# A four-layer graph network on one core: exps turned in 32x32 blocks by VectorE and brought to their keys' partitions by transfers

## The chip, the core and the metric

One core of a Trainium2 chip runs the whole program in a single launch. The metric is the device time of one execution in microseconds (us), as the median of several runs. The engines are TensorE (PE; its weight loads are listed as PEld), VectorE (DVE), ScalarE (ACT), GpSimd (POOL) and SyncE (SP), which here only issues transfers.

## The reference

x is (32, 512, 256) in fp32 and adj (32, 512, 512) in int32, the same adjacency for all four layers. Every layer adds to x a function of `h = max(layernorm(x), 0)`:

```python
# layer 0: 8 heads of 32
normed = layer_norm(h, gamma1, beta1)                       # q = k = v = normed, per head
attn = softmax(where(adj > 0, q @ k.T / sqrt(32), -inf))
h = h + attn @ v
out = h + gelu(layer_norm(h, gamma2, beta2) @ W1 + b1) @ W2 + b2
# layers 1 and 2: 4 heads of 64 (graph attention)
logits = leaky_relu(src_i + dst_j)                          # src, dst: one number per token and head
out = softmax(where(adj > 0, logits, very small)) @ (h @ W)
# layer 3: 4 heads of 64
q, k, v = h @ Wq + bq, h @ Wk + bk, h @ Wv + bv
out = relu(softmax(where(adj | eye, q @ k.T / 8, min)) @ v @ Wo + bo)
```

The 32 batches are independent of each other.

## The kernel before

**Work of a batch.** A batch holds its 512 tokens as four chunks of 128 partitions (token `c * 128 + q` in chunk c, partition q). Layers 0 and 3 share the helpers `attend` and `unit`. `attend` loops over two halves of the queries and over groups of heads (G = 4 heads in layer 0, G = 2 in layer 3, so that a group fills 128 partitions of q and k). For each chunk of 128 queries it issues the score products `dots` (L1078) into PSUM tiles pss, two heads in each, and then one `unit` per head:

- `masked` (L1125, VectorE): adds the mask to the 128x512 scores, negates, writes them to an SBUF tile e and keeps the row minimum in low;
- `exps` (L1137, ScalarE): the exp in place, with its row sum;
- `turn` (L1143, TensorE): four 128x128 transpositions of e into a PSUM tile pst, so that keys come to the partitions;
- `evacuate` (L963, VectorE or ScalarE): copies pst into eT.

When both query chunks of a half are there, `product` (L1099, TensorE) multiplies eT with the values into pso, and the `finish` of the layer divides by the row sums. A batch has 32 units in layer 0 and 16 in layer 3, 1536 in the whole run.

Layers 1 and 2 (`gat_layer`, `gat_attend`, `head_pair`, `gat_exps`) work with keys on partitions from the start; they need the mask transposed once per batch (maskT: `turn` in `batch`, L1747, four bf16 transpositions per chunk into psmT, copied out by VectorE at L1757). Their row maxima (junk, L1260) are VectorE's, their leaky exps (psu, e: L1446, L1467) ScalarE's, their sums over keys (esum, L1371) GpSimd's. Layer 0 ends with an MLP (psf L1528, psg L1549).

**Loads.** SP issues one transfer per 128 rows of adj (L1715, into one of two adj buffers), one for x (L1733) and one for the result (L1777). GpSimd turns each adj tile into a bf16 mask (L1720); this is done once for layers 0 to 2 and once more for layer 3.

**What sets the order.** All pieces of work are `Op`s of a `Plan`. Each has an engine (or a choice of two), a cost in the code, the buffers it needs and its predecessors. `Plan.schedule` places them one at a time: always the piece that can start first, and among those that can start at the same time the one with the smallest key. Up to four batches are in flight (FLIGHT). The finished list fixes each engine's instruction order; on the chip the engines only wait for each other by semaphores. The key is

```python
o.key = o.b * PACE + min(o.b, CHAINS - 1) * RAMP - o.cp - URGENCY.get(o.kind, 0.0)
fine = FINE.get(o.kind, ())
o.key -= fine[o.nth] if o.nth < len(fine) else 0
```

where cp is the longest path to the end and URGENCY and FINE are tables of numbers per kind of piece and per piece of a kind.

**Buffers.** PSUM: four tiles of one bank (tag one, for pst, pso and nearly all else) and two tiles of two banks (tag two: pss and psu). SBUF: six E tiles of 8 KB a partition (eT, the exps of layers 1 and 2, the MLP's hidden values), eight e tiles of 2 KB.

Of the kernel before, what the change touches and what calls it, by code (L numbers as in the profile page):

```python
# [9 lines left out]
F32 = mybir.dt.float32  # L10
# [6 lines left out]
P = 128  # L17
# [10 lines left out]
PACE = 24.3  # L28

RAMP = 466.5  # L30

LATENCY = {"PE": 0.25, "DVE": 0.18, "ACT": 0.26, "POOL": 0.15, "SP": 3.5}
TABLE_LOAD = 1.3

SWITCH = 150.8

SKEW = {"DVE": 0.07, "ACT": 0.0}
E_UNITS = 8

URGENCY = {  # L40
    "0:attend.dots:pss": 462.9,
    "0:attend.product:pso": -175.4,
    "0:batch:x": 178.5,
    "0:divide.scale:od": 938.2,
    "0:divide.turn:psd": 415.4,
    "0:divide:rc": 799.1,
    "0:evacuate:eT": 821.7,
    "0:evacuate:oT": -725.9,
    "0:finish.residual:h": -329.4,
    "0:layer0.down:psg": 1019.5,  # L50
    "0:layer0.rest:h": -1654.6,
    "0:layer0.up:psf": 35.3,
    "0:layer0:gT": 744.2,
    "0:layer0:h": -787.8,
    "0:layer0:x": 858.2,
    "0:mask_rows:adj": -575.2,
    "0:mask_rows:mask": -375.4,
    "0:moments.combine:mv": 317.1,
    "0:moments:st": 585.1,
    "0:norm:n": -2315.9,  # L60
    "0:norm:y": 27.1,
    "0:norm_relu:h": 451.8,
    "0:transposed.affine:qT": -614.7,
    "0:transposed.affine:yT": 1599.0,
    "0:transposed.turn:ps": 842.1,
    "0:unit.exps:e": -287.5,
    "0:unit.masked:e": 695.6,
    "0:unit.turn:pst": 906.7,
    "1:batch.turn:psmT": -364.5,
    "1:batch:maskT": -56.9,  # L70
    "1:divide.scale:od": 656.7,
    "1:divide.turn:psd": 1795.9,
    "1:divide:rc": -399.6,
    "1:evacuate:esum": -106.0,
    "1:evacuate:hT": 267.4,
    "1:evacuate:oT": -390.5,
    "1:gat_attend.key_terms:terms": 120.6,
    "1:gat_attend.maximum:grt": -949.2,
    "1:gat_attend:psd": 493.9,
    "1:gat_exps.leaky:psu": 254.7,  # L80
    "1:gat_exps.less:psu": 1557.1,
    "1:gat_exps.logits:psu": 232.7,
    "1:gat_exps:e": 1404.4,
    "1:gat_layer.project:psv": 1864.8,
    "1:head_pair.add:esum": 1941.4,
    "1:head_pair.product:pso": -781.0,
    "1:head_pair.sums:psz": 1214.9,
    "1:head_pair.turn:pst": -702.1,
    "1:head_pair:x": -1263.8,
    "1:largest.leaky:glz": 257.7,  # L90
    "1:largest:head": 34.7,
    "1:largest:most": 515.6,
    "1:largest:psm": 616.6,
    "1:largest:psn": 719.1,
    "1:moments.combine:mv": 1347.0,
    "1:moments:st": -193.6,
    "1:norm_relu:h": 564.8,
    "1:query_terms.terms:psw": 625.5,
    "1:rows_of.turn:psr": 520.6,
    "1:rows_of:rows": 297.3,  # L100
    "1:transposed.turn:ps": -474.0,
    "2:batch:mask": 20.7,
    "2:divide.scale:od": 1020.3,
    "2:divide.turn:psd": -785.5,
    "2:divide:rc": 718.1,
    "2:evacuate:esum": 268.7,
    "2:evacuate:hT": 67.8,
    "2:evacuate:oT": 2309.3,
    "2:gat_attend.key_terms:terms": 203.2,
    "2:gat_attend.maximum:grt": -1980.4,  # L110
    "2:gat_attend:psd": -581.1,
    "2:gat_exps.leaky:psu": -55.6,
    "2:gat_exps.less:psu": 277.3,
    "2:gat_exps.logits:psu": -221.2,
    "2:gat_exps:e": -803.2,
    "2:gat_layer.project:psv": -61.6,
    "2:head_pair.add:esum": 1765.9,
    "2:head_pair.product:pso": 275.0,
    "2:head_pair.sums:psz": -327.3,
    "2:head_pair.turn:pst": 571.6,  # L120
    "2:head_pair:x": 797.9,
    "2:mask_rows:adj": -580.1,
    "2:mask_rows:mask": -1055.3,
    "2:moments.combine:mv": 1499.2,
    "2:moments:st": 649.2,
    "2:norm_relu:h": -939.1,
    "2:query_terms.terms:psw": 256.8,
    "2:rows_of.turn:psr": 587.2,
    "2:rows_of:rows": -334.9,
    "2:transposed.turn:ps": 157.5,  # L130
    "3:attend.dots:pss": -1153.0,
    "3:attend.product:pso": -176.0,
    "3:batch:": -158.3,
    "3:evacuate:eT": -518.7,
    "3:evacuate:hT": -758.1,
    "3:evacuate:oT": 1394.4,
    "3:finish.spread:od": -316.9,
    "3:finish.turn:psr": 9.0,
    "3:finish:qT": -219.8,
    "3:finish:rc": -224.7,  # L140
    "3:layer3.biased:kT": 1662.2,
    "3:layer3.biased:qT": -462.4,
    "3:layer3.project:psk": -1285.4,
    "3:layer3.project:psq": 440.8,
    "3:layer3.project_v:psv": -300.3,
    "3:moments.combine:mv": 105.4,
    "3:moments:st": 752.7,
    "3:norm_relu:h": -4275.8,
    "3:project_out.add:x": 1996.5,
    "3:project_out.project:psw": -1291.9,  # L150
    "3:transposed.turn:ps": 397.0,
    "3:unit.exps:e": -287.1,
    "3:unit.masked:e": 592.5,
    "3:unit.turn:pst": -698.3,
}

FINE = {
    "0:attend.dots:pss": (
        26, 2, -1, -1, -1, -1, -36, -36,
    ),  # L160
    "0:attend.product:pso": (
        -123, -169, 83, -178,
    ),
    "0:batch:x": (
        30,
    ),
    "0:divide.scale:od": (
        5, -254, -116, 388,
    ),
    "0:divide.turn:psd": (  # L170
        -194, 3, -165, -57,
    ),
    "0:divide:rc": (
        -124, 16, -118, 9,
    ),
    "0:evacuate:eT": (
        0, -217, 4801, -188, 371, 176, 143, -381, 37, 119, 230, 185, 57, -46, -86, 139, -81, -15,
        223, -45, 59, -43, 177, 455, 45, -17, -12, 2, 25, -194, 118, -6,
    ),
    "0:evacuate:oT": (  # L180
        6, 84, -133, -26,
    ),
    "0:finish.residual:h": (
        -12, -60, -96, -130,
    ),
    "0:layer0.down:psg": (
        -80, -151, -109, 6,
    ),
    "0:layer0.rest:h": (
        -34, 51, -126, 13,  # L190
    ),
    "0:layer0.up:psf": (
        124, -172, -156, 145, -173, 64, -297, -184,
    ),
    "0:layer0:gT": (
        -105, -49, 42, -9, 115, -86, -50, 7,
    ),
    "0:layer0:h": (
        110, -95, -64, 31,
    ),  # L200
    "0:layer0:x": (
        13, 9, 37, 114,
    ),
    "0:mask_rows:adj": (
        -4, -1, 12, -36,
    ),
    "0:mask_rows:mask": (
        70, -58, -121, 69,
    ),
    "0:moments.combine:mv": (  # L210
        -12, 20,
    ),
    "0:moments:st": (
        -19, -48, 23, -89, -154, -179, -239, -171, -32, -164, -105, -82,
    ),
    "0:norm:n": (
        -4532, -4538, -4519, -4571,
    ),
    "0:norm:y": (
        -117, -26, -164, -223,  # L220
    ),
    "0:norm_relu:h": (
        -168, -276, -195, -261,
    ),
    "0:transposed.affine:qT": (
        -815, -106,
    ),
    "0:transposed.affine:yT": (
        361, 38,
    ),  # L230
    "0:transposed.turn:ps": (
        -593, -649, -208, -165,
    ),
    "0:unit.exps:e": (
        494, -41, 21, -71, -27, 264, 218, 1016, 80, -106, -66, -162, 18, -91, -63, -176, -53, 134,
        -47, -92, -85, -50, 167, 121, -99, -45, -70, -121, 50, 34, 55, -28,
    ),
    "0:unit.masked:e": (
        -10, -64, -87, -127, -385, -377, -391, -364, -60, -51, -7, -38, -165, -9, -142, 70, -29,
        -58, -31, -2, -78, -76, -40, -75, -4, 22, 20, 24, -118, -106, -28, -24,  # L240
    ),
    "0:unit.turn:pst": (
        -297, -422, -738, -401, -276, -253, -299, 296, 57, -188, 1, 62, -272, -298, 2, -35, -239,
        18, -238, -77, -117, -76, -36, -95, -133, -226, -214, -405, 89, -29, -208, -143,
    ),
    "1:batch.turn:psmT": (
        -17, 24, -128, -32,
    ),
    "1:batch:maskT": (
        2, -7, -50, 19,  # L250
    ),
    "1:divide.scale:od": (
        66, 88,
    ),
    "1:divide.turn:psd": (
        -665, -335,
    ),
    "1:divide:rc": (
        77, -7,
    ),  # L260
    "1:evacuate:esum": (
        -42, -22,
    ),
    "1:evacuate:hT": (
        19, 208, 73, -51, 41, 40,
    ),
    "1:evacuate:oT": (
        -81, -866,
    ),
    "1:gat_attend.key_terms:terms": (  # L270
        366,
    ),
    "1:gat_attend.maximum:grt": (
        19, 112, 80, 37, 18, -14, -6, 45, 61, -61, -21, 15, 7, 119, 26, 192,
    ),
    "1:gat_attend:psd": (
        -20, -173, -151, -188,
    ),
    "1:gat_exps.leaky:psu": (
        13, 172, -144, 229, 52, -342, -1019, -556,  # L280
    ),
    "1:gat_exps.less:psu": (
        -174, -58, -153, -180, -381, -613, 79, 311,
    ),
# [1532 lines left out]
```

## Time and profile before

| | |
|---|---|
| median of 3 runs | 5228.39 us (5225.8 to 5230.76) |
| the profiled execution | 5227.27 us, its span 5225.5 us, granted TensorE clock 0.991 |
| PEld busy | 2810.8 us |
| POOL busy | 2709.7 us (52%) |
| exps, L1137 on ACT | 1536, 1102.5 us busy, mean 724 ns |
| esum, L1371 on POOL | 384, of which 256 take 602.2 us, mean 2359 ns |
| mask from adj, L1720 on POOL | 256, 494.2 us busy, mean 1931 ns |
| mask turned, L1747 on PE | 512, 44.5 us busy |
| issues of x, adj and out on SP | 32, 256 and 32 |

Busy times are those of one profiled execution. The span runs from the first to the last instruction of the core; the execution's own time lies 1.77 us above it. Matmuls are pipelined, so their durations overlap: the busy time of a group is the union, its mean duration is that of a single one, and neither alone is what an instruction costs in a dense stream. A line number can be that of a helper: all copies out of PSUM made by `evacuate` have L963.

### The profile page before, as it was taken

Reading aid. Unit: us, or ns where it says so; the run is one execution under the profiler, and the core shown is the slowest. Engines: PE = TensorE matmul, PEld = TensorE weight load, DVE = VectorE, ACT = ScalarE, POOL = GpSimd, SP = SyncE. Lnnn points to the kernel's source line nnn. Section 1 sums busy time; section 2 is a strip of 40 time slices with the busy share of each in tenths; the row PEclk is TensorE's granted clock in tenths of the full one; section 3 lists DMA queues with packets and bytes.
Section 4 is the critical chain, followed back from the end, with each engine's and each line's share of the span. In section 5 each row is a group of like instructions: output and inputs, shape, how many; then the busy total and the mean of one; then the engine's idle time right before and its main releaser. Section 6 shows DMA issues by size and latency. Waiting matters only on the chain.

```text
span 5225.5 us, 86599 instructions
## 1 busy us (share of the span) xinstructions
PE 5085.6 (97%) x30972; PEld 2810.8 (54%) x30972; DVE 3163.1 (61%) x9219; ACT 3668.6 (70%) x7053; POOL 2709.7 (52%) x3988
## 2 busy tenths in 40 slices
PE   6989999999999999999999999999999999999998
PEld 4544555555555555555555555555555555555554
DVE  5545666666565666565666666665656665666653
ACT  6747777777677777677776667776777766677755
POOL 6445544565544655445655445654446554456442
PEclk9989999999999999999999999999999999999999
DMA  2000000000000000000000000000000000000000
GB/s 84 1 9 25 20 10 21 25 25 25 17 11 23 25 25 25 11 15 25 25 25 19 11 21 25 25 25 15 13 23 25 25 25 15 11 25 25 13 13 13
DMA packets 78692, 110.31 MB, mean 21 GB/s; under 512 B 9523, under 2 KB 45238, under 8 KB 78262
## 3 DMA queue, kind: packets, MB, share of 16 engines
q1 hardware_dynamic: 70656, 100.68, 6.4%
q8 instruction: 246, 4.03, 0.3%
q10 hardware_dynamic: 7606, 4.08, 0.3%
q14 instruction: 184, 1.51, 0.1%
HBM read 87.97 MB, written 16.78 MB: 20 GB/s over the span
## 4 chain that ended last, share of the span: by engine, by line
PE 76%; POOL 13%; DVE 5%; ACT 3%; issue 2%; DMA 0%; ACTq 0%; POOLq 0%; SPq 0%; DVEq 0%
PE pst L1143 12%; PE pss L1078 9%; PE psg L1549 8%; PE psf L1528 8%; PE pso L1099 8%; POOL esum L1371 6%; PE psv L1574 4%; PE pso L1385 4%; PE psu L1441 3%; POOL mask L1720 2%; PE psk L1597 2%; PE psv L1625 2%; DVE junk L1260 2%; PE psq L1597 2%; PE psu L1433 2%
## 5 line engine op out<-in xcount | busy, mean ns | idle before, releaser
L1137 ACT ACTIVATE e<-e,low 128x512 f32<-128x512 f32 x1536 | 1102.5, 724 | 143.8 <-DVE low L1125 136.5
L1125 DVE CUSTOM_DVE_ANT_0 e<-pss,mask 128x512 f32<-128x512 f32 x1536 | 985.3, 682 | 253.3 <-PE pss L1078 212.8
L1143 PE MATMUL pst<-ident,e 128*128 128x128 f32 x6144 | 854.1, 278 | 29.9 <-ACT eT L963 20.2
L1143 PEld LDWEIGHTS pst<-ident,e 128*128 128x128 f32 x6144 | 673.0, 141 | 370.2 <-ACT e L1137 193.3
L1260 DVE CUSTOM_DVE_ANT_0 junk<-psd,mask 128x512 bf16<-128x512 f32 x1024 | 702.5, 686 | 124.3 <-PE psd L1248 93.8
L1371 POOL TENSOR_TENSOR esum<-esum,e 128x1024 f32<-128x1024 f32 x256 | 602.2, 2359 | 51.6 <-ACT e L1467 42.2
L1446 ACT ACTIVATE psu<-psu 128x1024 f32<-128x1024 f32 x512 | 509.1, 1011 | 164.7 <-PE psu L1441 164.0
L963 ACT COPY eT<-pst 128x512 f32<-128x512 f32 x954 | 520.7, 590 | 113.6 <-PE pst L1143 110.7
L1467 ACT ACTIVATE e<-psu 128x1024 f32<-128x1024 f32 x512 | 513.9, 1025 | 34.7 <-PE psu L1450 32.4
L1720 POOL TENSOR_SCALAR mask<-adj_mask 128x512 bf16<-128x512 int32 x256 | 494.2, 1931 | 53.8 <-DVE low L1125 19.1
L983 POOL TENSOR_TENSOR mw_h<-st_h 128x4 f32<-128x4 f32 x128 | 26.1, 204 | 935.4 <-DVE st_h L974 934.1
L1385 PE MATMUL pso<-e,hT 128*64 128x512 f32 x2048 | 474.8, 606 | 0.0
L1528 PE MATMUL psf<-yT,w_L_gnn_W 128*128 128x512 f32 x1024 | 457.0, 596 | 0.8 <-ACT gT L1539 0.8
L1549 PE MATMUL psg<-w_L_gnn_W,gT 128*128 128x256 f32 x2048 | 448.3, 379 | 0.4 <-ACT gT L1539 0.4
L963 DVE COPY eT<-pst 128x512 f32<-128x512 f32 x582 | 386.1, 685 | 83.2 <-PE pst L1143 73.2
L1549 PEld LDWEIGHTS psg<-w_L_gnn_W,gT 128*128 128x128 f32 x2048 | 386.4, 190 | 53.5 <-ACT gT L1539 1.2
L1371 POOL TENSOR_TENSOR esum<-e 128x1024 f32<-128x1024 f32 x128 | 301.1, 2352 | 171.6 <-ACT e L1467 160.5
L1502 POOL TENSOR_TENSOR od<-od,b_L_gnn_gamma 128x256 f32<-128x256 f32 x128 | 93.4, 730 | 519.9 <-DVE od L1182 519.7
L1008 ACT ACTIVATE h<-x,mv_h 128x256 f32<-128x256 f32 x512 | 272.2, 594 | 74.8 <-POOL mv_h L994 41.8
L1441 PE MATMUL psu<-maskT,ident 128*128 128x512 bf16 x1024 | 316.2, 391 | 0.0
L1539 ACT ACTIVATE gT<-psf,c_L_gnn_b 128x512 f32<-128x512 f32 x256 | 175.3, 689 | 196.4 <-PE psf L1528 195.9
L1528 PEld LDWEIGHTS psf<-yT,w_L_gnn_W 128*128 128x128 f32 x1024 | 188.0, 190 | 227.9 <-issue 204.5
(192 smaller groups left out, 8355.7 us busy)
## 6 DMA issues: line engine op xcount, KB each, us to landing
adj_mask<-in_adj SPq DMA_DIRECT2D x256, 256.0 KB, 2.6
x<-in_x SPq DMA_DIRECT2D x32, 512.0 KB, 3.9
out<-x SPq DMA_DIRECT2D x32, 512.0 KB, 3.2
w_L_gnn_W<-in_L_gnn_W ACTq DMA_DIRECT2D x2, 1024.0 KB, 6.6
w_L_gnn_W<-in_L_gnn_W ACTq DMA_DIRECT2D x1, 256.0 KB, 7.2
w_L_gnn_W_proj<-in_L_gnn_W_proj ACTq DMA_DIRECT2D x1, 256.0 KB, 7.4
w_L_gnn_Wo<-in_L_gnn_Wo ACTq DMA_DIRECT2D x1, 256.0 KB, 7.7
w_L_gnn_Wq<-in_L_gnn_Wq ACTq DMA_DIRECT2D x1, 256.0 KB, 7.1
```

The source lines that it names most:

```text
L963: lambda e: (nc.scalar.copy if e == "ACT" else nc.vector.tensor_copy)(dst(), view(src.t)),
L1125: nc.vector.tensor_tensor_reduce(out=ex.t, in0=src.t[:, j, :], in1=mask.t[:, q, :], scale=-scale, scalar=FLT_MAX, op0=ALU.add, op1=ALU.min ...
L1137: nc.scalar.activation(ex.t, ex.t, AF.Exp, bias=low.t, scale=-1.0, accum_out=total.t[:, q, h : h + 1])
L1143: nc.tensor.transpose(ps.t[:, c, :], ex.t[:, bass.ts(c, P)], ident)
L1260: nc.vector.tensor_tensor_reduce(out=junk.t, in0=dB.t, in1=mask.t[:, q, :], scale=1.0, scalar=-FLT_MAX, op0=ALU.add, op1=ALU.max, accum_ou ...
L1371: nc.gpsimd.tensor_tensor(esum.t, left, es[c // 2].t[:, c % 2, :, :], ALU.add)
L1385: nc.tensor.matmul(o.t[bass.ts(j, GD), :], v.t[:, c, bass.ts(2 * p + j, GD)], es[c // 2].t[:, c % 2, j, :], start=(c == 0), stop=(c == NC ...
L1446: nc.scalar.activation(ps.t, ps.t, AF.Prelu, alpha=SLOPE)
L1467: lambda e: nc.scalar.activation(dst.t[:, c % 2, :, :], ps.t, AF.Exp),
L1528: nc.tensor.matmul(ps.t, w1[:, d, bass.ts(f, P)], yT.t[:, d, :], start=(d == 0), stop=(d == DC - 1),)
L1549: nc.tensor.matmul(ps.t, gT[f // (FC // 2)].t[:, f % (FC // 2), bass.ts(c, P)], w2[:, f, :], start=(f == 0), stop=(f == FC - 1),)
L1720: lambda e, at=at, c=c: nc.gpsimd.tensor_scalar(mask.t[:, c, :], at.t, 0, -BIG, op, ALU.mult),
```

## The change

**Turning the exps.** `unit` no longer has a TensorE step nor an evacuation. Four units (four heads of one query chunk) share an SBUF tile t of 8 KB a partition, laid out as blocks of 32 keys x units x 128. VectorE masks into it, ScalarE takes the exp in place, and VectorE transposes each 32x32 block in place (L841 of the new file). A block of keys then still lies on the partitions of its queries' block. A new step `move` brings it to its keys' partitions: SP issues 16 transfers, one for each pair of a query block and a key block, each of 32 partitions x 2 KB (64 KB), from t to eT. A batch has 8 moves in layer 0 and 4 in layer 3.

**Tokens in blocks of 32.** For the keys to come out in order, a chunk now holds tokens `k * 128 + c * 32 + i` (chunk c, partition `k * 32 + i`). So x, out and every adj tile are transferred in four pieces of 32 partitions, the scores and the row maxima read their moving operand through `by_blocks`, and the mask for layers 1 and 2 is turned by 16 small matmuls per chunk (32 columns of weights each) into an fp32 PSUM tile instead of four bf16 transpositions.

**Buffers.** E: three tiles of 16 KB in place of six of 8 KB (layer 3 now fills one tile for both groups of heads). t: three of 8 KB, in place of e. oT two in place of three, adj one in place of two; one pair of terms in place of two.

**Order.** URGENCY and FINE go; the key is `o.b * PACE + min(o.b, CHAINS - 1) * RAMP + START[o.kind][o.nth]` with a table START of wanted times per piece, and new values of PACE, RAMP, SWITCH and SKEW. A transfer now occupies SP in the plan for its whole cost.

```diff
-LATENCY = {"PE": 0.25, "DVE": 0.18, "ACT": 0.26, "POOL": 0.15, "SP": 3.5}
+LATENCY = {"PE": 0.25, "DVE": 0.18, "ACT": 0.26, "POOL": 0.15, "SP": 2.4}
...
             end = t + cost
-            free[e] = end if e != "SP" else t + 0.1
+            free[e] = end
...
+    def by_blocks(t):
+        return t.rearrange("p (c r i) -> p r c i", r=NB, i=BL)
...
 # attend
-            for g in range(H // G):
-                eT = [exp_tile([P, 2, NC, HQ * P], f"eT_{name}_{half}_{g}_{j}", b) for j in range(G // 2)]
+            for lead in range(0, H // G, 4 // G):
+                eT = exp_tile(f"eT_{nm}")
+                for s in range(HQ):
+                    q = half * HQ + s
+                    tb = Buf(att, [P, NB, 4, NC * BL], F32, "t", 3, f"t_{nm}_{s}")
...
-                                kT.t[r0 : r0 + dh, g, :],
+                                    by_blocks(kT.t[r0 : r0 + dh, g, :]),
...
+                    def move(e, s=s, tb=tb, eT=eT):
+                        for i in range(NB):
+                            for r in range(NB):
+                                nc.sync.dma_start(
+                                    eT.t[bass.ts(r, BL), s * NB + i, :],
+                                    tb.t[bass.ts(i, BL), r, :, :].rearrange("p u n -> p (u n)"),
+                                )
+                    plan.op(
+                        ("SP", 6.0), move, b, r=tb.parts(*range(4)), w=[eT[s]], alloc=[eT]
+                    )
...
-                                eT[j // 2].t[:, j % 2, c, :],
+                                    eT.t[:, :, bass.ts((u0 + j) * NC + c, BL)],
...
 # unit, after the exps
-        def turn(e):
-            for c in ALL:
-                nc.tensor.transpose(ps.t[:, c, :], ex.t[:, bass.ts(c, P)], ident)
...
-        plan.op(
-            ("PE", 0.5), turn, b, r=[ex[0]], w=[ps[0]],
-            alloc=[ps, dst],
-        )
-        evacuate(
-            lambda: dst.t[:, j, :, bass.ts(qs, P)], [dst[j, qs]], ps, nm, b, N
-        )
+        plan.op(("DVE", 0.68), lambda e: nc.vector.transpose(ex(), ex()), b, w=[tb[u]])
...
 # mask_rows
-            at = Buf(io, [P, N], I32, "adj", 2, f"adj_{tag}_{b}_{c}")
+            at = Buf(io, [P, N], I32, "adj", 1, f"adj_{tag}_{b}_{c}")
...
-                lambda e, at=at, c=c: nc.sync.dma_start(at.t, adj[b, bass.ts(c, P), :]),
+                lambda e, at=at, c=c: by_token(lambda k: nc.sync.dma_start(
+                    at.t[bass.ts(k, BL), :], adj[b, k * P + c * BL : k * P + (c + 1) * BL, :]
+                )),
...
 # batch, the mask turned for layers 1 and 2
-            ps = one(f"psmT_{b}_{c}", [P, N], BF16)
+            ps = one(f"psmT_{b}_{c}")
...
                 for q in ALL:
-                    nc.tensor.transpose(
-                        ps.t[:, bass.ts(q, P)], mask.t[:, q, bass.ts(c, P)], ident16
-                    )
+                    for k in range(NB):
+                        nc.tensor.matmul(
+                            ps.t[bass.ts(k, BL), bass.ts(q, P)],
+                            mask.t[:, q, k * P + c * BL : k * P + (c + 1) * BL],
+                            ident16,
+                            start=True,
+                            stop=True,
+                        )
```

## The prediction

> **What bounds the kernel now.** I read four views. First the page: busy times, the chain that ended last, and the costliest groups.
>
> ```profile
> PE 5085.6 (97%) x30972; PEld 2810.8 (54%) x30972; DVE 3163.1 (61%) x9219; ACT 3668.6 (70%) x7053; POOL 2709.7 (52%) x3988
> ...
> PE 76%; POOL 13%; DVE 5%; ACT 3%; issue 2%; DMA 0%; ACTq 0%; POOLq 0%; SPq 0%; DVEq 0%
> PE pst L1143 12%; PE pss L1078 9%; PE psg L1549 8%; PE psf L1528 8%; PE pso L1099 8%; POOL esum L1371 6%; PE psv L1574 4%; PE pso L1385 4%; PE psu L1441 3%; POOL mask L1720 2%; PE psk L1597 2%; PE psv L1625 2%; DVE junk L1260 2%; PE psq L1597 2%; PE psu L1433 2%
> ...
> L1125 DVE CUSTOM_DVE_ANT_0 e<-pss,mask 128x512 f32<-128x512 f32 x1536 | 985.3, 682 | 253.3 <-PE pss L1078 212.8
> L1143 PE MATMUL pst<-ident,e 128*128 128x128 f32 x6144 | 854.1, 278 | 29.9 <-ACT eT L963 20.2
> ...
> L963 ACT COPY eT<-pst 128x512 f32<-128x512 f32 x954 | 520.7, 590 | 113.6 <-PE pst L1143 110.7
> ...
> L963 DVE COPY eT<-pst 128x512 f32<-128x512 f32 x582 | 386.1, 685 | 83.2 <-PE pst L1143 73.2
> ```
>
> TensorE is busy 97% of the span and carries 76% of the chain; its largest single item is the one the change takes away, the transposition of the exps (pst).
>
> Then windows. One layer-0 down projection (psg) follows the last by 158.8 us ((5001.54 - 1031.59)/25 in the chain in order of time), so that is the period of a batch. I cut one into the attention half and the rest.
>
> ```profile
> 3026.00:3106.00 80.00, 79.96 (x489) 49.08 (x488) 52.09 (x159) 55.34 (x126) 28.44 (x50) 1.00 0.05 14
> 3106.00:3185.00 79.00, 77.00 (x478) 37.80 (x477) 47.13 (x131) 57.29 (x91) 55.75 (x75) 1.00 0.09 27
> ```
>
> The columns after the length are PE, PEld, DVE, ACT, POOL: TensorE works 157.0 of 159 us, and no other engine passes 73% in either half. Outside 31 periods the span holds 5225.5 - 31 x 158.8 = 302.7 us of start and drain.
>
> Third, the timeline, for what an instruction really takes of its engine (starts, since durations overlap).
>
> ```profile
> 3032.50 2.02 PE L1143 MATMUL pst<-ident,e 128*128 128x128 f32 x16
> 3034.45 1.14 PE L1078 MATMUL pss<-qT 32*128 32x512 f32 x8
> ...
> 3030.69 0.69 DVE L1125 CUSTOM_DVE_ANT_0 e<-pss,mask 128x512 f32<-128x512 f32 x1
> ...
> 3031.30 0.69 DVE L1125 CUSTOM_DVE_ANT_0 e<-pss,mask 128x512 f32<-128x512 f32 x1
> ```
>
> Sixteen transpositions advance TensorE by 1.95 us, 0.122 each; a VectorE pass over 512 columns takes 0.61 us from start to start.
>
> Fourth, the transfers.
>
> ```profile
> q1 hardware_dynamic: 70656, 100.68, 6.4%
> ...
> adj_mask<-in_adj SPq DMA_DIRECT2D x256, 256.0 KB, 2.6
> x<-in_x SPq DMA_DIRECT2D x32, 512.0 KB, 3.9
> ...
> L1715 SPq DMA_DIRECT2D adj_mask<-in_adj x256: 327/328/1585, 1.8 to 5127.8; - x128
> ...
> SPq L1715 <- POOL mask L1720: 4347.0, 202, 202.6
> ```
>
> A transfer costs SP 0.328 us to issue and lands after 2.6 us; SP otherwise sits waiting for GpSimd to free an adjacency buffer, so its queue is nearly empty.
>
> **Part by part, per batch (48 units, 12 moves).** Counts and places are from the two instruction orders.
>
> *Removed from TensorE:* 192 transpositions. By starts 192 x 0.122 = 23.4 us, by the row's busy time 854.1/32 = 26.7 us; I take 25. All of it lies on the bound.
>
> *Added to TensorE:* the mask's turn for layers 1 and 2 goes from 16 to 64 matmuls, each with its own weight load and a quarter of the output. The row before is 44.5/512 = 87 ns each; a new one lies between a quarter of that (64 x 0.022 - 1.4 = 0) and the whole (64 x 0.087 - 1.4 = +4.2 us). I take 60 ns, nearer the top because the weight load stays: +2.4 us. Scores and products now read their moving operand in runs of 32. The nearest row reads in runs of 128 (psq, 124.8/256 = 488 ns) against contiguous psf (457/1024 = 446 ns), 9%; on scores and products (577 + 499 us, 33.6 a batch) that would be +3.0 us. Psq also waits more for its input, so I take 0 and keep 3 for the top; a gain here I exclude, since no column is dropped.
>
> TensorE work: 157.0 - 25 + 2.4 = 134.4 us, with today's waits of 1.8 us 136.2.
>
> *VectorE and ScalarE:* 1536 evacuations go (520.7 us ACT, 386.1 us DVE), 1536 transpositions of 128x512 fp32 come, all on VectorE, in place. The trace has none. Nearest rows: the 128x512 fp32 pass, 0.61 us by starts; below, the one SBUF copy of that size that ran faster (waug, 427 ns); above, two passes, 1.22. I take 0.61. In the new order ScalarE takes over other copies (oT, esum, hT, qT, about 170 us) and VectorE drops about 190, and the mask copy grows from 419 to 685 ns (+34). Sums: DVE 3163 - 386 + 937 - 190 + 34 = 3558, ACT 3669 - 521 + 170 = 3318, both well under 32 x 134.4 = 4301. Averaged over the span nothing else binds.
>
> *The attention stage.* But the order gathers layer 0 of one batch and layer 3 of an older one into one stretch: from the first scores to the first layer-3 products TensorE has about 71 us of work, the rest 65 (each instruction at its row's busy time, times 0.9: such times sum to 150 us a batch for 134.4 of work, as neighbouring matmuls overlap). In that stretch VectorE has 48 x (0.61 + 0.61) = 58.6 us plus some 15 of divisions, statistics and copies; ScalarE 48 exps at 0.71 from start to start, 34 us, and about as much of leaky exps and copies; SP ten of the twelve moves. Four queues of nearly equal length, each in order: the stage is where a wait can show.
>
> *The moves.* Each is 16 transfers of 64 KB on SP, 6144 in the run. At 0.328 us plus 0.017 for the semaphore step, 0.35: 5.6 us a move, 2.6 us until the last lands (a smaller transfer should not land later than the 256 KB row; the 512 KB row, 3.9, is the upper end). Eight transfers are in flight at most in the order's waits, 2.6/8 = 0.33, the same pace. Bandwidth: q1 moved 100.68 MB in 6.4% of 16 engines, 301 GB/s while busy, so 64 KB needs 0.22 us, less than its issue. From the end of the last scores of a tile to its eT: four masked passes and four transpositions, 4.9 us, with a copy or reciprocal between them 5.2; last landing 5.6 + 2.6 = 8.2 us later; four hops from engine to engine, 0.4 in all: 13.8 us. TensorE work that the order puts in between: 11.4, 13.1, 16.1 and 12.0 us for the four eT of layer 0, 9.3 us for the first of layer 3, 40 for the second. Shortfalls: 2.4 at the first, which covers the second's 0.7, 1.8 at the fourth, 4.5 at layer 3's first: 8.7 us of new TensorE waits.
>
> The Trainium skill, "DMA: Bandwidth & Descriptors", speaks against this change: under Rules for kernel authors, transfers below 64 KB are mostly overhead and two copies to disjoint partition halves serialize; under Bandwidth, a 64 KB load takes 0.95 us. By that, as an estimate, sixteen in a row take 15.2 us, ten moves make the stage 163 us and the run some 7,400 us; the adjacency row's issue every 0.33 us with 2.6 us to landing shows transfers overlapping, so the sum goes by the row.
>
> *Queues passed.* Moves share SP with adjacency loads (four small ones each, one buffer instead of two), x and out. An adjacency load waits for GpSimd's mask pass (1.93 us); behind the layer-3 mask's loads stand the last two moves of layer 3, whose product has 40 us of TensorE work ahead of it: nothing, and some 2 us per load were that cover gone. A VectorE transposition waits for its exp with the next masked passes behind it, and the next scores wait for those; that is in the 14 us. Extra issues for x and out (8 a batch, 3 us of SP) fall into SP's idle time. The drain has no other batch to hide layer 3's moves: +15 us, one exposed chain.
>
> **Sum.** Period 136.2 + 8.7 = 144.9 us; 31 x 144.9 + 302.7 + 15 = 4810 us of span. The profiled run took 5227.27 us for a span of 5225.5 (+1.8), and the median of the runs is 1.1 above it: 4813, rounded 4810 us. Only over 0.2% (10 us) counts as a difference here.
>
> **Rivals.**
> *The waits vanish.* If landings are quicker than the load rows and the stage keeps 14 us of cover everywhere, the period is 136.2: 31 x 136.2 + 302.7 + 3 = 4528 us. For: TensorE waits almost nowhere today. Against: four queues of equal length. Chance 0.24.
>
> *SP becomes the bound, slower.* The mechanism is the price of one transfer on SP, its place the ten moves of the stage (164 transfers with one adjacency load). The stage takes 8 us to the first full tile, then 164 prices, then 2.6. With 65 us outside, it reaches 158.3 us, the break-even ((5225.5 - 317.7)/31), at (93.3 - 10.6)/164 = 0.50 us. At 0.61, as the small loads on ScalarE's queue at the start show, the stage is 110.6, the period 175.6 and the time 5760 us. For: 0.38 to 0.49 for x and out, and 3.9/8 = 0.49 were landing to set the pace. Against: 256 issues at 0.328. Chance 0.17, of which 0.11 slower, 0.02 level, 0.04 still faster.
>
> *VectorE becomes the bound.* Transpositions at two passes add 48 x 0.61 = 29 us: stage 103, period 168, 31 x 168 + 318 + 3 = 5530 us; break-even at (93.3 - 74)/48 + 0.61 = 1.0 us. Nothing in the trace speaks for it but that the operation is absent. Chance 0.09, half of it (0.05) slower.
>
> **How the numbers follow.** The forecast (4650 to 5000) has 0.50. Faster: 0.50 + 0.24 + 0.04 + 0.04 = 0.82; same 0.02; slower 0.16. The range goes from just under the waitless case, 4500, over the strided reads (+3 x 31 = 93) and doubled waits (8.7 x 31 = 270, together 5173), to 5190; above it lie most of both bound cases, 0.14, below 0.06.
>
> **What would show it.** Right: no pst rows; StreamTranspose near 0.6 to 0.7 us, moves at 0.35 us a transfer, TensorE at 92 to 95%, its waits at the products on DMA. Wrong: SP's issues above 0.5 us or back to back through the stage, transpositions over 1 us, waits of scores on masked passes larger than those on transfers, or a TensorE without gaps near 4530.

## The result and the profile after

The changed kernel takes 6629.5 us (median of 4 runs, 6622.0 to 6635.4) against 5227.2 us before (4 runs): a ratio of 1.268, 95% interval 1.266 to 1.270. It is slower by 1402 us. The forecast was 4810 us, and the rival "SP becomes the bound", at 5760, had the right sign and a chance of 0.17 (0.11 of it for a slower kernel).

The page of the changed kernel, in the order of the one before: busy times, the granted clock in 40 slices, the chain by engine and by line, three groups.

```profile
PE 5069.9 (76%) x26364; PEld 2415.3 (36%) x26364; DVE 3597.7 (54%) x9868; ACT 3340.8 (50%) x6396; POOL 2707.3 (41%) x3984
PEclk7778888888888888888887888888888888888887
SPq 41%; PE 29%; DVE 10%; issue 7%; DMA 6%; ACT 4%; POOL 3%; ACTq 0%; POOLq 0%; DVEq 0%
L820 DVE CUSTOM_DVE_ANT_0 t<-pss,mask 128x512 f32<-128x512 f32 x1536 | 995.6, 680 | 673.9 <-PE pss L764 522.1
L841 DVE STREAM_TRANSPOSE t<-t 128x512 f32<-128x512 f32 x1536 | 1013.3, 690 | 44.4 <-ACT t L836 43.1
L798 PE MATMUL pso<-eT,n 128*32 128x256 f32 x4096 | 408.8, 569 | 742.5 <-DMA eT<-t 629.5
```

Three things are to be seen. The chain has moved from TensorE to SP's queue: 41% of it is the time of issuing transfers. TensorE's largest idle time, 742.5 us, lies ahead of the products and ends with a move's landing. And TensorE has 4608 instructions fewer than before, yet its busy time is the same (5069.9 against 5085.6 us): the row PEclk shows why, the granted clock is 0.83 in the mean, where it was 0.991.

SP's own rows, from the answers on the two lines that issue transfers (duration of one as min/median/max in ns, first and last start):

```profile
L783 SPq DMA_DIRECT2D eT<-t x6144: 507/589/1937, 58.1 to 6614.5; - x199
L1402 SPq DMA_DIRECT2D adj_mask<-in_adj x1024: 310/420/1600, 18.7 to 6517.6; - x171
```

The move's line in the list of transfers (count, size, median us from issue to landing):

```profile
eT<-t SPq DMA_DIRECT2D x6144, 64.0 KB, 2.0
```

And SP's queue in the timeline, at the moves of one attention stage (start, length, count):

```profile
2193.40 106.99 SPq L783 DMA_DIRECT2D eT<-t  x160
```

A transfer of the move holds SP for 0.589 us in the median, and from start to start for 0.633 (192 of them: 121 us a batch). It lands after 2.0 us, sooner than I took. The ten moves of one attention stage run back to back for 107 us. One layer-0 down projection follows the last by 200.7 us ((1723.89 - 720.40)/5 in the chain in order of time). The windows cut one period at the first move of the stage (columns after the length: PE, PEld, DVE, ACT, POOL, the clock, DMA share, GB/s):

```profile
2100.00:2193.00 93.00, 86.26 (x445) 45.80 (x445) 52.58 (x156) 42.81 (x64) 46.88 (x60) 0.89 0.22 57
2193.00:2301.00 108.00, 71.50 (x380) 29.12 (x378) 59.82 (x153) 61.09 (x136) 37.41 (x64) 0.78 0.42 97
```

TensorE works 157.8 us of these 201, where the sum gave it 134.4. So two things went wrong: SP's price, and the length of TensorE's own work.

### The profile page after: what moved, and what is told of

It reads as the page before. It is cut to its first block, busy times and chain, and to the rows that moved or that the text cites. A ratio compares the mean times of both kernels' runs of the same rounds, so it can differ in the third digit from the quotient of the medians.

```text
span 6628.3 us, 88458 instructions
## 1 busy us (share of the span) xinstructions
PE 5069.9 (76%) x26364; PEld 2415.3 (36%) x26364; DVE 3597.7 (54%) x9868; ACT 3340.8 (50%) x6396; POOL 2707.3 (41%) x3984
## 4 chain that ended last, share of the span: by engine, by line
SPq 41%; PE 29%; DVE 10%; issue 7%; DMA 6%; ACT 4%; POOL 3%; ACTq 0%; POOLq 0%; DVEq 0%
SPq L783 39%; PE pso L798 6%; PE pso L1066 4%; DVE t L820 3%; PE pss L764 3%; DMA eT<-t 3%; DVE junk L941 3%; DMA adj_mask<-in_adj 3%; PE psg L1227 2%; PE psv L1252 2%; PE psf L1206 2%; SPq L1402 2%; PE psu L1121 2%; POOL mask L1409 2%; DVE t L841 2%
## 5 line engine op out<-in xcount | busy, mean ns | idle before, releaser
L836 ACT ACTIVATE t<-t,low 128x512 f32<-128x512 f32 x1536 | 1097.8, 716 | 714.0 <-DVE low L820 578.6
L820 DVE CUSTOM_DVE_ANT_0 t<-pss,mask 128x512 f32<-128x512 f32 x1536 | 995.6, 680 | 673.9 <-PE pss L764 522.1
L841 DVE STREAM_TRANSPOSE t<-t 128x512 f32<-128x512 f32 x1536 | 1013.3, 690 | 44.4 <-ACT t L836 43.1
L798 PE MATMUL pso<-eT,n 128*32 128x256 f32 x4096 | 408.8, 569 | 742.5 <-DMA eT<-t 629.5
L1066 PE MATMUL pso<-e,hT 128*64 128x512 f32 x2048 | 557.1, 694 | 4.1 <-DVE maskT L1454 3.9
L798 PEld LDWEIGHTS pso<-eT,n 128*32 128x32 f32 x4096 | 191.7, 155 | 955.8 <-issue 862.3
L798 PE MATMUL pso<-eT,hT 128*64 128x256 f32 x2048 | 313.8, 467 | 234.0 <-DMA eT<-t 138.9
L764 PE MATMUL pss<-qT 32*128 32x512 f32 x2048 | 373.2, 724 | 36.9 <-DVE low L820 27.4
L764 PE MATMUL pss<-kT,qT 64*128 64x512 f32 x1024 | 311.7, 705 | 112.3 <-DVE low L820 112.2
L640 ACT COPY oT<-pso 128x256 f32<-128x256 f32 (+1 forms) x200 | 101.6, 508 | 569.3 <-PE pso L798 312.3
```

Source lines behind the costliest of these rows:

```text
L764: nc.tensor.matmul(tiles[i // 2].t[:, i % 2, :], qT.t[r0 : r0 + dh, g, bass.ts(q, P)], by_blocks(kT.t[r0 : r0 + dh, g, :]), start=True, st ...
L798: nc.tensor.matmul(o.t[bass.ts(j, dh), :], v.t[:, c, bass.ts(g * G + j, dh)], eT.t[:, :, bass.ts((u0 + j) * NC + c, BL)], start=(c == 0), ...
L820: nc.vector.tensor_tensor_reduce(out=ex(), in0=src.t[:, j, :].rearrange("p (r n) -> p r n", r=NB), in1=mask.t[:, q, :].rearrange("p (r n) ...
L836: lambda e: nc.scalar.activation(ex(), ex(), AF.Exp, bias=low.t, scale=-1.0, accum_out=total.t[:, q, h : h + 1]),
L841: plan.op(("DVE", 0.68), lambda e: nc.vector.transpose(ex(), ex()), b, w=[tb[u]])
L1066: nc.tensor.matmul(o.t[bass.ts(j, GD), :], v.t[:, c, bass.ts(2 * p + j, GD)], es.t[:, 2 * c + j, :], start=(c == 0), stop=(c == NC - 1),)
```

## The experiments

The theories: **1**, SP pays a fixed price per transfer, whatever its size, and the attention stage waits for SP; **2**, the bytes or the 32-partition form set the price; **3**, traffic around it does; **4**, the order of the work is at fault. Theories on the rest came up with the first results. Runs without an interval are single executions, beside a run of the kernel before at 5228 to 5232 us.

**Prices alone.** A kernel of transfers, one form after the other.

> A kernel of transfers alone, back to back in groups: SBUF to SBUF with 32 rows of 2 KB (the move's form), of 1 KB and of 8 KB, with 128 rows of 2 KB; from DRAM with 32 and with 128 rows of 2 KB; a write of 1 MB to DRAM and reads of 256 KB back; the move's form again on ScalarE's and on GpSimd's queue. It computes nothing of the reference. Theory 1, a fixed price per issue: every SBUF-to-SBUF form holds SP for 0.59 us (0.63 from start to start) whatever its size, and the form from DRAM is the cheaper one, 0.33 to 0.43 us, with 32 rows as with 128. Theory 2, rows or bytes set the price: the 1 KB rows cost about half of the 2 KB rows (0.3 us), the 8 KB rows and the 128 rows about four times as much (2.4 us). Theory 3, the price comes from the surroundings (other engines' traffic in the changed kernel): alone on the chip the move's form costs 0.33 us like the adjacency loads of the kernel before.

```profile
L29 SPq DMA_DIRECT2D s2s_32x<-src x64: 507/589/1090, 3.0 to 91.5; - x64
L38 SPq DMA_DIRECT2D s2s_128x<-src x8: 470/600/1234, 93.4 to 98.9; - x8
L48 SPq DMA_DIRECT2D load_32x<-in_x x32: 356/419/424, 114.2 to 128.5; - x32
L54 SPq DMA_DIRECT2D load_128x<-in_x x8: 350/432/433, 130.7 to 134.0; - x8
L61 SPq DMA_DIRECT2D back_128x<-hb x8: 512/1434/2515, 139.3 to 149.2; - x8
L29 POOL DMA_DIRECT2D pool_32x<-src x32: 496/498/628, 185.7 to 201.0; - x32
```

The x64 are 32 transfers of 2 KB rows and 32 of 1 KB rows: both 0.589 us. 128 rows cost as much (0.600), 8 KB rows 0.656. From DRAM the price is 0.42 to 0.43 us, with 32 rows as with 128, and 0.35 for the first of a group, which finds the queue empty. GpSimd issues the move's form in 0.50 us, ScalarE in 0.60. Theories 2 and 3 fall for the form of the move: its price depends on the two memories and on whether issues follow each other, hardly on size. One form does not fit: of eight reads of 256 KB from a scratch in DRAM (L61), the first four took 0.51 to 0.71 us and the next four 2.2 to 2.5; why stays open. (The first group ran beside a copy of x to the output: after seven issues SP stood still for 47 us, and then went on at 0.633 us from start to start; the prices are the medians.)

**Fewer and more transfers with the same bytes.** In `move`:

```
# e2, 8 a move                                  # e3, 4 a move
for i in (0, 2):                                for r in range(NB):
  for r in range(NB):                             dma(eT[r, s*NB : s*NB+4], t[r, r] read 4 times)
    dma(eT[r, s*NB+i : s*NB+i+2], t[i, r] read twice)
# e4, 32 a move: as in the change, each transfer cut into two of 1 KB rows
```

> The changed kernel with 8 transfers a move in place of 16, each writing two query blocks from one source block: as many bytes are written, and half of the blocks are copies of their neighbour instead of their own data. Order and everything else as in the changed kernel. Theory 1 (price per transfer): a move holds SP for 8 x 0.63 = 5.1 us, which is what my sum had assumed (5.6), so if the rest of that sum holds the period is 145 us and the time about 4800 us. Theory 2 (bytes): a move still takes 10 us, the time stays at 6630 us. Theory 4 (the order and the clock are to blame, not SP): it stays above 6000 us.

> The changed kernel with 4 transfers a move, each writing all four query blocks from one source block (as many bytes written, three quarters of the blocks are copies of another). Theory 1: a move holds SP for 2.5 us, the transfers leave the bound altogether, and the time lies between the waitless 4530 and 4800 us, about 4650. Theory 2 (bytes): 6630 us. Theory 4 (order, clock): above 6000 us.

> The changed kernel with 32 transfers a move of half the size (32 rows of 1 KB), all data moved. Theory 1 (price per transfer): a move takes 20.2 us of SP, the ten of the attention stage 203 us in place of 107, so the period grows from 201 to about 297 us and the time to 31 x 297 + 400 = 9600 us. Theory 2 (bytes): 6630 us, since the bytes are the same.

Measured: 8 transfers 5361.3 us (ratio 1.026, 1.023 to 1.029), 4 transfers 5353.5 us (1.024, 1.021 to 1.027), 32 transfers 10385.9 us. All three lie above what theory 1 gave before they ran (4800, 4650 and 9600). With as many bytes, the number of issues alone moves the time from 5353 to 10386: theory 1 holds in this. But below 8 nothing more is gained, and 5353 is 540 us above my forecast, though a move then holds SP for about 3 us (four transfers of 256 KB, 0.70 us each in the median) in place of the 5.6 that the sum had assumed. SP explains 1268 us of the miss of 1820 (6629.5 - 5361.3); 1039 of them are idle time of TensorE (1558.4 - 519.3) and 228 its busy time (5069.9 - 4841.5). A second cause stands behind the rest.

**Half of the transfers from GpSimd.** All data are moved.

```
-  nc.sync.dma_start(
+  (nc.sync if i < 2 else nc.gpsimd).dma_start(
```

> The changed kernel with half of each move's 16 transfers issued by GpSimd in place of SP; all data moved, the order of everything else as in the changed kernel. Theory 1 (SP's price per transfer sets the attention stage, and a second limit near 5350 us lies behind it, as the runs with 8 and 4 transfers showed): SP needs 8 x 0.63 = 5.1 us a move and GpSimd 8 x 0.50 = 4.0 us, GpSimd works 84 + 48 = 132 us of a period of 160, and the time is 5350 to 5550 us. Theory 2 (bytes in flight set the pace of a move): 6630 us. Rival (GpSimd stands in order behind VectorE's turns, and its masks and sums come late): above 5700 us.

Measured 5677.5 us (1.086, 1.083 to 1.089): 952 us better than the change, 316 worse than with 8 transfers, between theory 1 and its rival. GpSimd is busy 75% of the span (4230.0 us), 1527.2 of it issuing.

**The planner told the measured price.** `("SP", 6.0), move` becomes `("SP", 10.2), move`.

> The changed kernel with one number changed: the planner takes 10.2 us for a move in place of 6.0, so the order is laid out for the price that was measured. Theory 1 (SP's 192 transfers of a batch are what counts, most of them in one stage): the sum of SP's work stays 121 + 17 us a batch, and the time 6400 to 6700 us. Theory 4 (the order is at fault, SP is free for a third of a period): other work is put beside the moves, and the time falls to 5400 to 6000 us.

Measured 6892.2 us, worse than the change and above what either theory gave: with the table of wanted times as it is, an order laid out for the true price does not find room for 121 us of issues beside the rest. This run gives theory 4 no support; a table of wanted times searched anew for the true price was not tried, so a better order is not ruled out.

**VectorE's turns left out** of the kernel with 4 transfers.

> The kernel with 4 transfers a move (5353 us), its VectorE transpositions left out as well; the order is kept. Theory V (the second limit is VectorE: masked passes and turns in line, so that scores wait): VectorE loses 48 x 0.66 = 32 us a batch and the time falls to my forecast's level, 4700 to 4900 us. Theory C (the second limit is TensorE with a lower clock and its waits on ScalarE's exps in layers 1 and 2): it stays at 5200 to 5350 us.

Measured 5342.0 us against 5353.5, with VectorE at 50% in place of 67%: its turns are not the second limit there. The granted clock stays at 0.902, as with 4 transfers. In that kernel, with 4 transfers a move, windows of 4 us show where it falls, in the stretch of layer 2 (columns as above):

```profile
2088.00:2092.00 4.00, 3.58 (x28) 1.79 (x25) 3.59 (x18) 1.50 (x5) 1.92 (x1) 1.00 0.22 54
2096.00:2100.00 4.00, 2.88 (x15) 0.91 (x14) 3.97 (x8) 4.00 (x7) 3.75 (x5) 0.77 0.00 0
2100.00:2104.00 4.00, 3.06 (x10) 0.82 (x12) 2.31 (x6) 3.41 (x4) 2.22 (x3) 0.50 0.77 145
2104.00:2108.00 4.00, 4.00 (x14) 1.23 (x12) 1.92 (x7) 1.18 (x3) 3.84 (x3) 0.50 1.06 234
```

and TensorE's timeline has the same score products twice in this stretch:

```profile
2103.04 2.99 PE L764 MATMUL pss<-qT 32*128 32x512 f32 x8 [0.32 <-ACT e L1147]
...
2110.75 1.14 PE L764 MATMUL pss<-qT 32*128 32x512 f32 x8
```

Eight products take 2.99 us in the cold stretch and 1.14 us 8 us later. Half the clock alone would make 2.28 of the 1.14; what adds the rest is open. No wait of TensorE there is longer than 1.2 us, and none between 1000 and 4500 us of that kernel longer than 2.2.

**TensorE's transpositions alone taken away, in the kernel before.** No transfer is added and no order changed; three of the four transpositions of a unit go.

```
 def turn(e):
-    for c in ALL:
-        nc.tensor.transpose(ps.t[:, c, :], ex.t[:, bass.ts(c, P)], ident)
+    nc.tensor.transpose(ps.t[:, 0, :], ex.t[:, 0:P], ident)
 # evacuate reads ps.t[:, 0:1, :] four times
```

> The kernel before, in its own order, with one of the four transpositions of each unit done and three left out (the copy out of PSUM reads the one four times): TensorE loses 48 x 3 x 0.122 = 17.6 us a batch, and nothing else changes. My sum's first step (all of TensorE's work lies on the bound, so what goes from it goes from the period): period 141.2 us, time 31 x 141.2 + 300 = 4680 us. Theory C (once TensorE has gaps, its waits on ScalarE in layers 1 and 2 come up and its granted clock falls there, so part of the gain is given back): 4900 to 5150 us, with the granted clock below 0.96.

```profile
PE 4811.2 (93%) x26364; PEld 2368.1 (46%) x26364; DVE 3146.7 (61%) x9219; ACT 3638.0 (70%) x7053; POOL 2708.7 (52%) x3988
PE 47%; POOL 24%; ACT 16%; DVE 8%; issue 4%; DMA 0%; ACTq 0%; POOLq 0%; DVEq 0%
```

Measured 5191.9 us (0.993, 0.991 to 0.995): 37 us for 17.6 us a batch taken from the busiest engine. Both theories expected more. TensorE's busy time fell by only 274 us: by starts a transposition in a dense run costs 0.122 us, but one standing alone is listed with 0.27 (415.9 us for 1536, where 6144 took 854.1), and the clock is 0.972. Its idle time grew by 245 us (5195.9 - 4811.2, against 139.9). GpSimd's and ScalarE's shares of the chain rise from 13% and 3% to 24% and 16%: with the same order, other engines' chains stood close behind TensorE. The order had been laid out for the old work; a new one for the smaller work was not tried here.

**ScalarE's leaky passes left out** of the kernel with 4 transfers (`leaky` does nothing).

> The kernel with 4 transfers a move (5353 us), with the leaky passes of layers 1 and 2 on ScalarE left out (16 a batch of 1.0 us); the order is kept. Theory C (the second limit is the hand-over between TensorE and ScalarE in the stretch of layer 2, where each logits tile takes a ScalarE pass, a short product and a second pass, and where TensorE's short waits bring its clock to 0.5): the time falls by more than the 16 us a batch that ScalarE loses would give if it were the bound by itself only at times, to 4800 to 5050 us, with the clock above 0.94. Rival (the limit is TensorE's own work or GpSimd's sums): above 5250 us.

Measured 5261.4 us, clock 0.908: 92 us, close to the rival. Theory C as I put it, with ScalarE's hand-over as the cause of the waits, falls.

**What lowers the clock.** Three kernels of matmuls alone.

> A kernel of fp32 matmuls 128x128 by 256 columns alone, in bursts of 4, 9, 18 or 36, each burst waiting for a short chain on VectorE that waits for the burst before (pauses of about 0.6, 0.9, 1.6 and 3 us), with a dense stretch of 100 matmuls ahead of each pattern; it computes nothing of the reference. Theory C (many short waits lower the granted clock): in patterns where TensorE works under some three quarters of the time the clock falls to about 0.5 and a matmul takes 0.43 us in place of 0.22, although no pause is longer than 1 us; long bursts with the same pause keep 1.0. Rival (only one long pause lowers the clock): all patterns but the last keep 1.0.

> Matmuls alone as in the run on pauses, but with longer pauses against shorter bursts: fp32 128x128 by 128 columns in bursts of 9, 18 and 36 with pauses of 0.4 to 4 us, then bf16 matmuls with 9 rows in a dense stretch and in bursts with pauses; 150 dense matmuls ahead of each pattern. Theory C: patterns in which TensorE works under about 80% of the time over some 6 us show a granted clock of 0.5 for several us and matmuls of twice the time, with pauses of 1 us as well, while patterns above 85% keep 1.0. Rival (it is the 9-row products that lower the clock, not the waits): the dense stretch of 9-row products falls to 0.5 too, and the fp32 patterns keep 1.0 up to pauses of 3 us.

> Matmuls alone again, dense, 512 columns, ahead of each pattern 24 fp32 matmuls of 128 rows: bf16 with 9, 32, 64, 96 and 128 rows, with 128 rows of which 119 hold zeros, fp32 with 32 and 64 rows and with 128 rows by 32 columns of weights, 9-row and 128-row bf16 products in turn; then fp32 of 128 rows in bursts of 2, 4 and 8 with pauses on a chain of VectorE copies of 1 to 5 us. Theory R (the clock follows how many rows of the array are fed, however dense the stream): 9 and 32 rows run at 0.50 throughout, 128 rows at 1.0, with a limit between; zeros count as rows; 9 and 128 in turn keep 1.0. Theory P (the clock follows waits alone): every dense pattern recovers to 1.0 and only the bursts with pauses fall.

In the first, the pauses came out at 0.3 us, since VectorE's copies ran beside the bursts: everything kept 1.0, and it settles little. The second had pauses of 0.5 us, everything of 128 rows kept 1.0, and a dense stretch of 9-row products fell to 0.50 and stayed there. The third, timeline of TensorE (the form is rows*columns of the weights, then rows x columns streamed):

```profile
25.79 29.66 PE L40 MATMUL d<-v,w 9*128 9x512 bf16 x80 [0.49 <-DVE v L47]
79.82 29.12 PE L40 MATMUL d<-v,w 32*128 32x512 bf16 x80 [0.49 <-DVE v L47]
132.18 17.44 PE L40 MATMUL d<-v,w 64*128 64x512 bf16 x80 [0.49 <-DVE v L47]
210.31 17.44 PE L40 MATMUL d<-v,w 128*128 128x512 bf16 x80 [0.49 <-DVE v L47]
249.38 17.44 PE L40 MATMUL d<-v,z 128*128 128x512 bf16 x80 [0.49 <-DVE v L47]
288.24 63.57 PE L37 MATMUL d<-v,w 32*128 32x512 f32 x80 [0.27 <-DVE v L46]
374.57 34.60 PE L37 MATMUL d<-v,w 64*128 64x512 f32 x80 [0.27 <-DVE v L46]
486.73 39.85 PE L40 MATMUL d<-v,w 9*128 9x512 bf16 x80 [0.49 <-DVE v L47]
```

and its windows of 10 us (columns as above, without ACT) in a dense 9-row stretch, in 9-row and 128-row products in turn, in bursts of 2 us with pauses of 1.6 us, and with pauses of about 3 us between bursts of 8 products (3.7 us at full clock) and of 16 (7 us):

```profile
40.00:50.00 10.00, 10.00 (x25) 3.41 (x24) 0.00 (x0) 0.00 (x0) 0.50 1.01 328
...
500.00:510.00 10.00, 10.00 (x20) 1.90 (x19) 0.00 (x0) 0.00 (x0) 0.50 0.00 0
...
620.00:630.00 10.00, 5.21 (x11) 1.84 (x11) 4.95 (x12) 0.00 (x0) 1.00 0.00 0
...
760.00:770.00 10.00, 6.96 (x12) 2.79 (x11) 3.03 (x6) 0.00 (x0) 0.72 0.00 0
...
870.00:880.00 10.00, 6.95 (x17) 2.94 (x16) 3.03 (x6) 0.00 (x0) 1.00 0.00 0
```

Streams on 9 rows (bf16) and on 32 rows (bf16 and fp32) fall to 0.50 within a few us and stay, though TensorE never pauses; 64 and 128 rows keep 1.0; rows that hold zeros count as rows (`d<-v,z`, 119 of 128 rows zero: 17.4 us for 80, the same). The last line is 40 products of 9 rows and 40 of 128 in turn, listed by the first form; it fell as well, which theory R had wrong. Pauses of 1.6 us do no harm even where TensorE works only half of the time; pauses of 3 us bring it down some of the time. So both rows and long pauses lower the clock, and waits of 1 us, which I had suspected, do not.

The Trainium skill, "TensorE: Matmul & The Clock Gate", Part 1, gives half the clock as the state of an idle array, entered after an idle window of about 3.4 us. Pauses of up to 1.6 us, which did no harm here, fit that; pauses of 3.05 us, a little below its figure, lowered the clock at times. The streams of 9 and 32 rows do not: no pause, and 0.50 throughout. Going by that page, the second limit would have been looked for in the waits alone.

**The same in the kernel.** In the kernel with 4 transfers, the products of layers 1 and 2 that read 9 rows (logits and less) read more:

```
-  rk.t[r0 : r0 + 9, bass.ts(c, P)], rq.t[r0 : r0 + 9, :]      # and minus, likewise
+  e13: [r0 : r0 + 32]      e14: [0 : 128]
```

> The kernel with 4 transfers a move (5353 us), its 9-row products of layers 1 and 2 (logits and less) read 32 rows, of which 23 hold zeros; same results of these layers, same order. Theory R with a limit above 32 rows: no change, 5340 to 5360 us. With a limit below 32 rows: clock above 0.95 and the time 5100 to 5250 us.

> The same with 128 rows in these products (the terms of the four heads are summed, so layers 1 and 2 compute something else). Theory R: the stretch of layers 1 and 2 keeps a clock near 1.0, the mean clock rises from 0.90 to 0.97 or more, and the time falls by what the slow matmuls cost less what returns as waits: 5000 to 5200 us. Theory P (waits lower the clock): no change, 5340 to 5360 us.

Measured 5349.8 us with 32 rows (clock 0.903) and 5209.2 us with 128 (clock 0.960). As in the kernel of matmuls alone, 32 rows change nothing and 128 do: 144 us come back, although the wider products do not run beside each other as the narrow ones did and are listed with more time (619 us in place of 456 for the two groups). By the trace's clock records TensorE is busy at half the clock for 906 us of the kernel with 4 transfers and for 303 of this one; at half speed that loses 453 and 151 us. So rows account for two thirds of the loss there; what lowers the clock in the last third is open.

**What is left.** The kernel with 128 rows, without the leaky passes, without VectorE's turns, and without both.

> The kernel with 4 transfers a move and 128 rows in the products of layers 1 and 2 (5209 us), ScalarE's leaky passes left out (16 a batch of 1.0 us). Theory A (ScalarE's two passes per logits tile are the chain behind TensorE): 4850 to 5000 us. Theory N (no single engine, many chains in a fixed order): 5100 to 5200 us.

> The same kernel (5209 us) with VectorE's 48 turns a batch left out instead. Theory V (VectorE is the chain behind TensorE, hidden before by the low clock): below 5050 us. Theories A and N: 5150 to 5210 us.

> The same kernel with both left out. If ScalarE and VectorE hold each other's place: below 4900 us though each alone gives little. Theory N: still above 5050 us.

Measured 5122.1, 5156.8 and 5056.1 us. Each gives a little, both together about the sum (153 us, where 87 and 52 make 139), and none reaches the forecast: theory N. Which chain holds the rest stays open.

None of the runs that came out below the kernel before (e9, e14 to e17; e14 and e9 by less than 1%) does all of the computation; of those that do, the one with two queues comes closest, 8.6% behind.

## Why the prediction was wrong

TensorE's busy time and idle time make up the span, so each step can be set against its own number. The forecast's busy time is 134.4 x 31 + (5085.6 - 157.0 x 31) = 4385 us, its idle time the other 425 of 4810.

| | TensorE busy | idle | clock | time |
|---|---|---|---|---|
| before | 5085.6 | 139.9 | 0.991 | 5227 |
| forecast | 4385 | 425 | not in the sum | 4810 |
| 8 transfers a move | 4841.5 | 519.3 | 0.899 | 5361 |
| 4 transfers, 128 rows | 4700.5 | 506.9 | 0.960 | 5209 |
| the change | 5069.9 | 1558.4 | 0.830 | 6630 |

**The step that failed: "At 0.328 us plus 0.017 for the semaphore step, 0.35: 5.6 us a move".** It measured 0.633 and 10.1 us. The price was taken from adjacency loads, which come from DRAM, one at a time, into an idle queue; the move's transfers go from SBUF to SBUF, back to back. Both differences cost: 0.35 to 0.43 us for following each other, 0.43 to 0.59 for the memories. The other rows at hand (0.38 to 0.49 for x and out, 0.61 for small loads) were kept for the rival, and the row with the largest count was taken, where the row nearest in kind was wanted. This step is 1268 us, nine tenths of the way from 5227 to 6630. It does not decide the sign by itself: with 8 transfers a move the kernel is still 2.6% slower.

**A step that was missing: the granted clock.** "TensorE work: 157.0 - 25 + 2.4 = 134.4 us" counts every matmul at its row's duration, at a clock of 0.991. With SP relieved (8 transfers) the busy time is 456 us above the sum. By the trace's clock records 1084 us of that run stood at 0.50, and TensorE was busy for 945 of them, a loss of about 473 us at half speed, against 35 in the kernel before. Busy time less this loss is 4369 us, against 4385 in the sum: the clock is the whole excess, and the work itself was counted rightly. There is some luck in that, since the transpositions gave back about 22 us a batch in place of 25 (5085.6 - 35 - 4369 over 32 batches, with 0.4 for the mask's turn), and the mask cost 0.4 in place of 2.4. That few rows lower it is shown (matmuls alone, and 144 us in the kernel with 128 rows); that the transpositions, which feed 128 rows, had kept the clock up between the 9-row and 32-row products before is argued from this, not shown by itself. In the change, waits of up to 17 us for moves come on top, and the clock is 0.83 (1428 us busy at 0.50, a loss of about 714): TensorE's 750 us of transpositions (6144 x 0.122) are gone and its busy time is where it was.

**What held.** VectorE's transposition: 0.59 to 0.63 us by starts, where 0.61 was taken. VectorE 3597.7 us and ScalarE 3340.8 against sums of 3558 and 3318. The landing 2.0 us, under the 2.6. Strided reads cost nothing: eight scores still take 1.14 us at full clock. The mask's turn was overpaid: 32 matmuls take 0.9 us, so 64 cost 0.4 us more than before, not 2.4. The waits, 425 us in the sum, were 519 with 8 transfers, so the idle step was short by 94 us.

**The rivals.** SP as the bound was named with its mechanism, its place and its break-even of 0.50 us, and the price of 0.61 that it put there was nearly the one measured. At 0.633 its formula gives a stage of 8 + 164 x 0.633 + 2.6 = 114 us, a period of 179 and 5880 us; 6630 came, because both parts were longer. From a batch's first scores to the next products of layer 3 passed 125 us in the trace (2176.7 to 2302.2: 16.7 to the first move in place of 8, 107 for the ten moves, 1.8 to the landing), and outside them 76 us in place of 65. VectorE did not bind. "The waits vanish" would not have come to 4528 even with free transfers: 5353. The rule that the prediction quoted from the Trainium skill, "DMA: Bandwidth & Descriptors", spoke against the change and had the sign right; its 0.95 us a transfer (estimate 7,400 us) was as far above the measured 0.633 as the adjacency row was below. The same page, under Issuing engines are not separate DMA queues, calls the sequencer's time for starting a transfer usually small beside the transfer: here it decided (6630 to 5677 us by a second issuing engine).

**Work taken from the engine that is 97% busy.** The rival's floor and the forecast both let the period fall by all that TensorE lost. The run on the kernel before gives 1.2 us a batch (37/31) for 17.6 us of it. A busy share of 97% and a chain that is 76% TensorE say that TensorE limits; they do not say how far behind the next chain stands.

## What to carry to other kernels

Take the price of an issue from a row of the same kind, same pair of memories and same spacing, and multiply it by the count for each stage: many small transfers from one queue are an engine's work like any other. Before counting on time freed on the busiest engine, take that work away by itself in a trial and see what the period does. When full-array matmuls go from between products on few rows, look at the granted clock first: the products left behind may take twice their time.

## What the runs showed of the hardware

- One issue on SP: SBUF to SBUF 0.59 to 0.60 us with 32 rows of 1 or 2 KB or 128 rows of 2 KB (0.63 from start to start in the kernel); DRAM to SBUF 0.42 to 0.43 us in a row, 0.35 on an empty queue, but 2.2 to 2.5 us in the second half of eight reads of 256 KB from a scratch (open). The same SBUF form costs ScalarE 0.60 and GpSimd 0.50 us.
- A 32x32-block transposition of 128x512 fp32 in place on VectorE costs 0.59 to 0.63 us from start to start, where another pass of that size (L1125 in the kernel before) takes 0.61.
- The granted clock of TensorE falls to 0.50 in an unbroken stream of products on 9 or 32 rows and stays at 1.0 on 64 and 128; 9-row and 128-row products in turn fall too (0.50); pauses of 1.6 us leave it at 1.0, pauses of 3.05 us gave 0.72 to 1.0.
